# A routed block-sparse FFN on Trainium2: the last batch element routed one tile earlier, its scatters and the output gathers re-planned

## The chip, the cores and the metric

The kernel runs on one core of one Trainium2 chip. The metric is the time of the kernel on the device in microseconds (us). Three runs of the kernel before gave 1059.44, 1061.75 and 1058.58 us; the median is 1059.44. One further execution was recorded by the hardware profiler; all views below come from it.

## What is computed

The input x has 16 batch elements of 512 tokens with 512 features. Each element first goes through a conditional layer, then through a feed-forward network of which each token uses 4 of 16 blocks, and the result is added to x.

```python
# conditional layer; v = u = fside (rank 16), per batch element
z1 = einsum('bfi,bir->bfr', x, v[:, 0]) / inch
z  = einsum('bfr,bor->bfo', z1, u[:, 0]) / r
g  = gelu(x @ W.T + fc_bias + z + cond)          # exact gelu
# routed feed-forward network: 16 blocks of 128 hidden units
prob = softmax(g @ w_router + b_router)
mask = (one for each of the 4 largest of prob, else zero)   # 16 wide
h = relu(einsum('nd,ebd->neb', g, w1b) + b1b)
y = einsum('neb,ebd,ne->nd', h, w2b, mask) + b2
out = x + y
```

All of it is float32. A kernel need not compute the 12 blocks that a token doesn't use.

## The kernel before

**Two stages and two lists in HBM.** Stage 1 computes g for one batch element after the other, decides which four blocks each token takes, and writes each token's row of g (2 KB) four times into `g_d`, once into the list of each block that it takes. A place in a list is called a slot. Stage 2 walks over the lists in tiles of 128 slots (`T`): it fetches a tile of `g_d`, multiplies it with the weights of its one block, and writes 128 rows of results to `y_d` at the same slots. For each chunk of 128 tokens, it then gathers the four result rows of each token from `y_d`, adds them, b2 and x, and stores the output. There are 271 tiles (`NT` = 16 per element and 15 for lists that don't end on a tile's edge) and 64 chunks (four per element).

**Stage 1** is `window(b)` (line 578), one call per element b, in eight half steps h. In each, `cond_half` issues two of the element's 16 large products; between them stand the next element's preparation and the routing of the element before, a = b - 1: `logits_in`, `logits`, `route_in` (softmax's exponential), `route_a` to `route_c` (the four largest, their mask), `turn_g` (the four transposes of g that give token rows, into buffers `gr`), `rank` and `place` (the slot numbers). Larger table work is put in as chores (line 601). The scatters of element b - 2, 16 indirect DMAs from POOL's queue (GpSimd), are issued two per half step by `put` (line 445). Each waits for the product issued last before it (`after`, line 453), so that they are spread over the products.

**Stage 2** is the loop of line 782, one step i per tile. Its body issues `fetch(i + 4)`, `turn(i + 1)` (transposes the tile on TensorE), `first(i)` (product with w1, relu on ScalarE), `second(i - 1)` (product with w2, copy on ScalarE, store to `y_d`) and `pick(i + 2)` (VectorE copies the tile's weights out of `wall`), and then what a hand-made plan, the dictionary `work`, holds for step i. `plan(step, ...)` fills it (line 726). `mark[0]` is always the last product that `first` issued (line 656). The order of PE, VectorE and ScalarE is the order of the code; the queue of SP carries fetches, stores of y and stores of the output, ScalarE's queue the x loads, POOL's queue all scatters and gathers.

What the plan holds:

- The last element z = 15 has no later window, so its routing is planned over steps -1 to 5 (line 744). When all slots are known, `count` and `ends` work out the lists' lengths, two last table parts and `table` (steps 8 to 10) give the rows and blocks of tiles 22 and up.
- The scatters of elements 14 and 15 (line 751): 14's at steps 0 to 7, 15's at steps 8 to 15, two per step. Then five `put_zero` DMAs at steps 16 and 17 clear the ends of the lists.
- Tiles 0 to 21 (`AHEAD` = 22) are full tiles of the first four elements; their fetches don't wait for scatters of later elements (line 633). The fetch of tile 22, issued in step 18, waits for all scatters and zero writes.
- Output chunk n (1 to 64; `b`, `c` in the code) may be gathered when the tiles below `begun` = max(38, 4n + 15) are stored (line 677). Its first step `at` is at least `begun + 3` and at least 4 (`TOP_K`) after the chunk before (line 731): 4n + 37. At `at + j` stands `get_y` (line 691), gather j of four, into buffers `yg`; there are six, of two gathers each. From `at + 3` on follow `sum_b`, the sums `sum_y` and `sum_x` on VectorE at `at + 4` to `at + 7`, and the output store at `at + 7`. The x rows are loaded (`load_x`, line 682) at the step max(at - 24, soon), into 11 buffers `xa` and `xb`; a buffer is free when the output store of the chunk 11 earlier has landed. The last two elements' x stays in SBUF and is not loaded again.

A gather waits for its buffer and for the stores of y that its chunk needs (lines 700 to 703), and for nothing else.

Of the kernel before, what the change touches and what calls it, by code (L numbers as in the profile page):

```python
# [19 lines left out]
TOP_K = 4  # L20
# [5 lines left out]
def adaln_ffn_kernel(  # L26
# [31 lines left out]
    B, S, D = x.shape  # L58
# [8 lines left out]
    Q = 4  # L67
# [5 lines left out]
    NTC = -(-(NT - AHEAD) // P)  # L73
# [16 lines left out]
    SYNC = mybir.DependencyInfo(mybir.DependencyClass.Sync, mybir.DependencyReason.DATA)  # L90

    def alone(ins):

        tc.declare_no_dep(ins.ins, group="put_g", reason="disjoint rows of the lists")
        tc.declare_no_dep(ins.ins, group="get_g", reason="the tiles that run ahead are full")
        tc.add_to_no_dep_group("put_g", ins.ins)
# [158 lines left out]
    def cond_half(b, h):  # L255

        o = h // 2
        if h % 2 == 0:
            pms[o] = ps_m.tile([P, S], F32, tag="m", name=f"pc_{b}_{o}")
        for k in range(h % 2 * ND // 2, (h % 2 + 1) * ND // 2):  # L260
            ins = nc.tensor.matmul(  # L261
                pms[o], lhsT=wes[b][:, k, o * P : (o + 1) * P], rhs=xTs[b, k], start=(k == 0), stop=(k == ND - 1)
            )
        if h % 2:
            gelu(b, o, pms[o])
        return ins
# [178 lines left out]
    def put(b, c, j, after):  # L445

        ins = nc.gpsimd.indirect_dma_start(  # L447
            out=g_d[:, :],
            out_offset=bass.IndirectOffsetOnAxis(ap=slot[:, b, c, j : j + 1], axis=0),
            in_=grs[b, c].bitcast(I32),  # L450
            in_offset=None,
        )
        tc.add_manual_dep(ins.ins, after.ins.name, SYNC, reason="spread over the products")
        alone(ins)
        if b < Q:
            early.append(ins.ins)
# [42 lines left out]
    def put_zero(i, after):  # L499
        ins = nc.gpsimd.indirect_dma_start(  # L500
            out=g_blocks if i else g_d[:, :],
            out_offset=bass.IndirectOffsetOnAxis(ap=zero_i[:, i : i + 1], axis=0),
            in_=(zero if i else zero[:, 0:D]).bitcast(I32),
            in_offset=None,
            bounds_check=NSLOT // ZB - 1 if i else NSLOT - 1,
            oob_is_err=False,
        )
        tc.add_manual_dep(ins.ins, after.ins.name, SYNC, reason="spread over the products")
        alone(ins)
# [60 lines left out]
    chores = {Q + 1: [(fill,), (count, 0, True)], Q + 2: [(take,), (table_ahead,)]}  # L570
    for q in range(B // Q - 1):
        chores.setdefault(Q * q + Q + (3 if q == 0 else 1), []).append((count, q))
    parts_of = [(table_part, 1, i, h, B // Q) for h in range(B // Q) for i in range(NTC)]
    known = NTC * (B // Q - 1)
    for k in range(known):
        chores.setdefault(B - 2 + k // 3, []).append(parts_of[k])

    def window(b):
        a = b - 1
        do = [[] for _ in range(2 * ND)]  # L580
        if b + 1 < B:
            do[0] += [(weights, b + 1)]
            do[2] += [(turn_x, b + 1, 0), (turn_x, b + 1, 1)]
            do[4] += [(turn_x, b + 1, 2), (turn_x, b + 1, 3)]
            if b > 0:
                do[1] += [(logits_in, a)]
                do[3] += [(logits, a), (route_in, a)]
                do[4] += [(route, a)]
                do[5] += [(turn_g, a, 0), (turn_g, a, 1)]
                do[6] += [(turn_g, a, 2), (turn_g, a, 3)]  # L590
                do[7] += [(rank, a), (place, a)]
            if b + 2 < B:
                do[2] += [(spread_v, b + 2)]
                do[5] += [(turn_v, b + 2), (turn_v_out, b + 2)]
        else:
            do[0] += [(logits_in, a)]
            do[1] += [(logits, a), (route_in, a)]
            do[2] += [(turn_g, a, 0), (turn_g, a, 1), (route, a)]
            do[3] += [(turn_g, a, 2), (turn_g, a, 3)]
            do[5] += [(rank, a), (place, a)]  # L600
        for h, what in zip((1, 3, 6), chores.get(b, ())):
            do[h] += [what]
        for h in range(2 * ND):
            ins = cond_half(b, h)
            for what, *args in do[h]:
                what(*args)
            if b > 1:
                for j in (0, 1):
                    put(b - 2, h // 2, h % 2 * 2 + j, ins)
            if later:  # L610
                what, *args = later.pop(0)
                what(*args)
# [4 lines left out]
    rows, gts, wcs, gss, hTs, mark, stores = {}, {}, {}, {}, {}, {}, []  # L617
# [59 lines left out]
    def begun(b, c):  # L677

        n = b * NC + c + 1
        return max(AHEAD + E, n * PB // NC + E - 1)  # L680
# [10 lines left out]
    def get_y(b, c, j):  # L691
        if j % 2 == 0:
            ygs[b, c, j // 2] = ygp.tile([P, 2, D], F32, tag="yg", name=f"yg_{b}_{c}_{j}")
        ins = nc.gpsimd.indirect_dma_start(  # L694
            out=ygs[b, c, j // 2][:, j % 2, :].bitcast(I32),
            out_offset=None,
            in_=y_d[:, :],
            in_offset=bass.IndirectOffsetOnAxis(ap=slot[:, b, c, j : j + 1], axis=0),
        )
        new = stores[begun(b, c - 1) if b + c > 0 else 0 : begun(b, c)]  # L700
        tc.declare_no_dep(ins.ins, group="put_y", keep=new, reason="later tiles have no slot of this chunk")
        for p in new:
            tc.add_manual_dep(ins.ins, p.name, SYNC, reason="its rows")
        tc.keep_in_program_order(ins)
        tc.add_to_no_dep_group("get_y", ins.ins)

# [14 lines left out]
    GAP = 3  # L721
# [4 lines left out]
    def plan(step, *what):  # L726
        work.setdefault(step, []).append(what)

    for b in range(B):
        for c in range(NC):  # L730
            at = max(begun(b, c) + GAP, at + TOP_K if b + c else 0)
            k = b * NC + c
            soon = FREE - 2 * XA + 2 * k if k < XA else FREE + 4 + k - XA
            plan(soon if k < XA + XB else max(at - 24, soon), load_x, b, c)
            for j in range(TOP_K):
                plan(at + j, get_y, b, c, j)
            plan(at + LAND, sum_b, b, c)
            for h in range(2):
                plan(at + LAND + 1 + 2 * h, sum_y, b, c, h)
                plan(at + LAND + 2 + 2 * h, sum_x, b, c, h)  # L740
            plan(at + LAND + 4, store, b, c)


    z = B - 1
    for step, *what in (
        (-1, logits_in, z), (0, logits, z), (0, route_in, z), (1, turn_g, z, 0), (1, turn_g, z, 1), (1, route_a, z),
        (2, route_b, z), (2, turn_g, z, 2), (3, route_c, z), (3, turn_g, z, 3), (4, rank, z), (5, place, z),
        (6, count, B // Q - 1), (7, ends), *((8 + k, *w) for k, w in enumerate(parts_of[known:])), (8 + NTC, table, 1),
    ):
        plan(step, *what)  # L750
    for i in range(NC * TOP_K):
        for k, b in enumerate((z - 1, z)):
            plan(8 * k + i // 2, lambda b, c, j: put(b, c, j, mark[0]), b, i // TOP_K, i % TOP_K)
    for i in range(1 + NZ):
        plan(16 + i // 3, lambda i: put_zero(i, mark[0]), i)

    ENG = mybir.EngineType
    with tc.manual_schedule(engines={ENG.PE, ENG.DVE, ENG.Activation}):
# [10 lines left out]
        for b in range(B):  # L769
            if 2 <= b + 2 < B:  # L770
                load(b + 2)
            window(b)
# [76 lines left out]
```

## Time and profile before

| what | value |
|---|---|
| three runs, median | 1059.44 us (1058.58 to 1061.75) |
| profiled execution | 1086.83 us, its span 1085.1 us |
| granted clock of TensorE, mean | 0.967 |
| busy share of the span: PE, PEld, DVE, ACT, POOL | 89%, 59%, 60%, 48%, 51% |
| DMA | 342.43 MB, 316 GB/s over the span |
| HBM read, written | 179.91 MB, 163.32 MB |
| first product of tile 0, of tile 22, of tile 270 | 392.01, 469.33, 1046.91 us |
| first gather of results, last one issued | 512.34, 1074.77 us |

PE is TensorE's products, PEld its weight loads, DVE is VectorE, ACT ScalarE, POOL GpSimd, SP the engine that only issues DMAs. PE's busy share overstates its work, since products are pipelined and their ends modelled. In a stage's row the DMA share is the mean busy share of the 16 DMA engines; it can come out a little above 1. "Idle before, releaser" behind a group of instructions tells how long its engine stood still just before them and what ended most of that. The chain is followed back from the last instruction, at each step to what released it; its lines give the start, the length and the instruction.

The three queues of DMAs in the page: SP's queue (fetches, y stores, output stores) took 48.1% of the engines' time over the span, POOL's (scatters, gathers) 33.6%, ACT's (x loads) 4.1%.

### The profile page before, as it was taken

How to read it: one execution, taken by the hardware profiler on the slowest of the kernel's cores; microseconds unless marked ns; L12 is line 12 of the kernel's file. 1: busy time of each engine (PE TensorE's matmuls, PEld its weight loads, DVE VectorE, ACT ScalarE, POOL GpSimd, SP SyncE). 2: the span in 40 equal slices, each digit the busy share in tenths (PEclk: the TensorE clock that was granted, in tenths of full speed). 3: DMA queues.
4: the chain of work that ended last, by engine and by line, in shares of the span. 5: the costliest groups of instructions: out<-in, count | busy, mean ns of one | idle time of the engine just before them, and what ended most of it. 6: DMA issues, size and time to landing. Idle time of an engine off the chain costs nothing.

```text
span 1085.1 us, 19007 instructions
## 1 busy us (share of the span) xinstructions
PE 970.9 (89%) x5320; PEld 639.3 (59%) x5320; DVE 648.0 (60%) x1450; ACT 518.8 (48%) x1006; POOL 550.3 (51%) x538
## 2 busy tenths in 40 slices
PE   5998988988999888789799999999999999999960
PEld 3544444544444455567577677677767777777740
DVE  4365667566556767323366666566666666666675
ACT  2333332342333434456466666566656566666640
POOL 2046666666666667500454445455444454444555
PEclk9999999999999988989899999999999999999985
DMA  9966667566654469988799999999999999999996
GB/s 301 332 230 216 224 215 261 208 225 242 226 223 179 170 224 318 358 265 272 259 382 405 394 388 403 391 394 395 395 397 401 395 396 398 380 405 398 392 354 211
DMA packets 161480, 342.43 MB, mean 316 GB/s; under 512 B 28723, under 2 KB 36951, under 8 KB 159046
## 3 DMA queue, kind: packets, MB, share of 16 engines
q1 hardware_dynamic: 110928, 188.53, 48.1%
q0 software_dynamic: 41856, 136.96, 33.6%
q10 hardware_dynamic: 8592, 15.73, 4.1%
q8 instruction: 44, 0.72, 0.3%
q14 instruction: 60, 0.49, 0.1%
HBM read 179.91 MB, written 163.32 MB: 316 GB/s over the span
## 4 chain that ended last, share of the span: by engine, by line
PE 58%; DMA 19%; DVE 8%; issue 5%; ACT 3%; POOL 2%; SPq 2%; another core or an unknown queue 2%; ACTq 1%; DVEq 0%; POOLq 0%
PE pc L261 17%; DMA gt<-g_d 14%; PE ph L656 14%; PE py L666 13%; PE pts L649 6%; PE ptx L248 2%; PE ptg L357 2%; PE pw L241 2%; PE pa L285 1%; ACT gs L650 1%; PE pl L294 1%; DVE xT L250 1%; DMA yg<-y_d,slot 1%; POOL g_d L447 1%
## 5 line engine op out<-in xcount | busy, mean ns | idle before, releaser
L694 POOL DMA_INDIRECT yg<-y_d,slot x256 | 283.1, 1106 | 338.0 <-DVE xr L715 163.8
L643 DVE COPY wcur<-wall 128x1028 f32 x271 | 193.0, 713 | 271.1 <-PE py L666 164.0
L447 POOL DMA_INDIRECT g_d<-gr,slot x256 | 254.3, 993 | 185.2 <-issue 65.8
L656 PE MATMUL ph<-gs,wcur 128*128 128x128 f32 x2168 | 293.7, 279 | 17.7 <-ACT gs L650 9.8
L666 PE MATMUL py<-wcur,h 128*128 128x512 f32 x542 | 281.2, 601 | 5.5 <-ACT h L660 4.8
L656 PEld LDWEIGHTS ph<-gs,wcur 128*128 128x128 f32 x2168 | 266.8, 194 | 26.6 <-ACT gs L650 17.4
L261 PE MATMUL pc<-xT,we 128*128 128x512 f32 x512 | 246.3, 608 | 0.0
L649 PEld LDWEIGHTS pts<-ident,gt 128*128 128x128 f32 x1084 | 134.9, 143 | 165.2 <-issue 108.8
L667 ACT COPY y<-py 128x512 f32<-128x512 f32 x271 | 159.2, 587 | 94.0 <-PE py L666 69.5
L650 ACT COPY gs<-pts 128x512 f32<-128x512 f32 x271 | 160.0, 590 | 85.0 <-DMA gt<-g_d 39.6
L649 PE MATMUL pts<-ident,gt 128*128 128x128 f32 x1084 | 165.6, 276 | 16.4 <-DMA gt<-g_d 14.3
L660 ACT ACTIVATE h<-ph,wcur 128x128 f32<-128x128 f32 x271 | 100.0, 369 | 89.6 <-PE ph L656 43.0
L261 PEld LDWEIGHTS pc<-xT,we 128*128 128x128 f32 x512 | 88.4, 192 | 88.7 <-issue 88.7
L270 ACT ACTIVATE gT<-pc,biasT 128x512 f32<-128x512 f32 x64 | 44.0, 688 | 158.0 <-PE pc L261 101.8
L712 DVE TENSOR_TENSOR yg<-yg 128x512 f32<-128x512 f32 x128 | 87.3, 682 | 8.2 <-DMA yg<-y_d,slot 6.8
L666 PEld LDWEIGHTS py<-wcur,h 128*128 128x128 f32 x542 | 83.2, 194 | 6.8 <-ACT h L660 5.1
L250 DVE COPY xT<-ptx 128x512 f32<-128x512 f32 x64 | 42.0, 686 | 60.4 <-PE ptx L248 27.8
L715 DVE TENSOR_TENSOR xr<-xr,yg 128x512 f32<-128x512 f32 x112 | 76.6, 684 | 0.0
L357 PE MATMUL ptg<-ident,gT 128*128 128x128 f32 x256 | 37.8, 281 | 27.1 <-issue 9.8
L357 PEld LDWEIGHTS ptg<-ident,gT 128*128 128x128 f32 x256 | 30.0, 143 | 50.5 <-issue 24.9
L243 DVE TENSOR_TENSOR we<-pw,wc 128x512 f32<-128x512 f32 x64 | 40.1, 683 | 23.9 <-PE pw L241 16.2
L248 PEld LDWEIGHTS ptx<-ident,x 128*128 128x128 f32 x256 | 31.3, 146 | 18.3 <-issue 14.9
(159 smaller groups left out, 511.2 us busy)
## 6 DMA issues: line engine op xcount, KB each, us to landing
gt<-g_d SPq DMA_DIRECT2D x271, 256.0 KB
y_d<-y SPq DMA_DIRECT2D x271, 256.0 KB
x<-in_x_dram SPq DMA_DIRECT2D x16, 1024.0 KB
xr<-in_x_dram ACTq DMA_DIRECT2D x56, 256.0 KB
out_dram<-xr SPq DMA_DIRECT2D x56, 256.0 KB
wall<-in_w1T_dram SPq DMA_DIRECT2D x16, 256.0 KB
wall<-in_w2T_dram SPq DMA_DIRECT2D x16, 256.0 KB
g_d<-gr,slot POOLq DMA_INDIRECT x256
```

The costliest lines, as they stand in the source:

```text
L261: ins = nc.tensor.matmul(pms[o], lhsT=wes[b][:, k, o * P : (o + 1) * P], rhs=xTs[b, k], start=(k == 0), stop=(k == ND - 1))
L357: nc.tensor.transpose(pt[:, k, :], gTs[b, k][:, c * P : (c + 1) * P], ident)
L447: ins = nc.gpsimd.indirect_dma_start(out=g_d[:, :], out_offset=bass.IndirectOffsetOnAxis(ap=slot[:, b, c, j : j + 1], axis=0), in_=grs[b, ...
L643: nc.vector.tensor_copy(wcs[i], wall_f[:, bass.DynSlice(w, WW)])
L649: nc.tensor.transpose(pt[:, k, :], gts[i][:, k * P : (k + 1) * P], ident)
L650: nc.scalar.copy(gs.rearrange("p k t -> p (k t)"), pt.rearrange("p k t -> p (k t)"))
L656: mark[0] = nc.tensor.matmul(ph, lhsT=wcs[i][:, k * P : (k + 1) * P], rhs=gss[i][:, k, :], start=(k == 0), stop=(k == ND - 1))
L660: nc.scalar.activation(h, ph, AF.Relu, bias=wcs[i][:, ND * P : ND * P + 1])
L666: nc.tensor.matmul(py, lhsT=hTs[i], rhs=wcs[i][:, ND * P + 4 : WW], start=True, stop=True)
L667: nc.scalar.copy(y, py)
L694: ins = nc.gpsimd.indirect_dma_start(out=ygs[b, c, j // 2][:, j % 2, :].bitcast(I32), out_offset=None, in_=y_d[:, :], in_offset=bass.Indir ...
L712: nc.vector.tensor_tensor(yg[:, 0, :], yg[:, 0, :], yg[:, 1, :], ALU.add)
```

## The change

- The routing of element 15 begins earlier: both logit steps and the exponential in step -1, the rest in steps 0 to 3, so that `place` comes in step 3 instead of 5; `count`, `ends`, the table parts and the table come one step earlier.
- The four scatters of element 14's first chunk are issued in the last window, in its last two half steps. The other 12 stand at steps 0 to 3, three per step. Element 15's stand at steps 4 to 11, the zero writes at steps 12 and 13.
- Of the six table parts that are done in windows 14 and 15, window 14 takes four instead of three; the fourth stands in half step 7.
- Chunks are at least 3 steps apart instead of 4, so `at` becomes max(4n + 18, 3n + 38); the four gathers of a chunk stand at `at`, `at`, `at + 1`, `at + 2`.
- Each gather waits in addition for the last product of `first` in its step.

```diff
-        chores.setdefault(B - 2 + k // 3, []).append(parts_of[k])
+        chores.setdefault(B - 2 + k // 4, []).append(parts_of[k])
...
-        for h, what in zip((1, 3, 6), chores.get(b, ())):
+        for h, what in zip((1, 3, 6, 7), chores.get(b, ())):
...
             if b > 1:
                 for j in (0, 1):
                     put(b - 2, h // 2, h % 2 * 2 + j, ins)
+                if b == B - 1 and h >= 6:
+                    for j in (0, 1):
+                        put(a, 0, h % 2 * 2 + j, ins)
...
             tc.add_manual_dep(ins.ins, p.name, SYNC, reason="its rows")
+        tc.add_manual_dep(ins.ins, mark[0].ins.name, SYNC, reason="spread over the products")
         tc.keep_in_program_order(ins)
...
-            at = max(begun(b, c) + GAP, at + TOP_K if b + c else 0)
+            at = max(begun(b, c) + GAP, at + 3 if b + c else 0)
...
-                plan(at + j, get_y, b, c, j)
+                plan(at + 3 * j // TOP_K, get_y, b, c, j)
...
-        (-1, logits_in, z), (0, logits, z), (0, route_in, z), (1, turn_g, z, 0), (1, turn_g, z, 1), (1, route_a, z),
-        (2, route_b, z), (2, turn_g, z, 2), (3, route_c, z), (3, turn_g, z, 3), (4, rank, z), (5, place, z),
-        (6, count, B // Q - 1), (7, ends), *((8 + k, *w) for k, w in enumerate(parts_of[known:])), (8 + NTC, table, 1),
+        (-1, logits_in, z), (-1, logits, z), (-1, route_in, z), (0, route_a, z), (0, turn_g, z, 0),
+        (1, route_b, z), (1, turn_g, z, 1), (1, turn_g, z, 2), (2, route_c, z), (2, turn_g, z, 3),
+        (3, rank, z), (3, place, z), (5, count, B // Q - 1), (6, ends),
+        *((7 + k, *w) for k, w in enumerate(parts_of[known:])), (7 + NTC, table, 1),
...
-        for k, b in enumerate((z - 1, z)):
-            plan(8 * k + i // 2, lambda b, c, j: put(b, c, j, mark[0]), b, i // TOP_K, i % TOP_K)
+        if i >= TOP_K:
+            plan((i - TOP_K) // 3, lambda b, c, j: put(b, c, j, mark[0]), z - 1, i // TOP_K, i % TOP_K)
+        plan(4 + i // 2, lambda b, c, j: put(b, c, j, mark[0]), z, i // TOP_K, i % TOP_K)
...
-        plan(16 + i // 3, lambda i: put_zero(i, mark[0]), i)
+        plan(12 + i // 3, lambda i: put_zero(i, mark[0]), i)
```

## The prediction

> **What bounds the kernel now.** I read the page's 40 slices first, then the busy time by stage, cut where the slices change, then the chain that ended last around each hole, then the timelines of POOL, ACT and SP. The stages (core 0: us, busy time and instructions of PE, PEld, DVE, ACT, POOL, then granted clock, DMA share, GB/s):
>
> ```profile
> 438.00:455.00 17.00, 16.89 (x106) 12.38 (x104) 5.10 (x7) 10.09 (x21) 12.26 (x12) 1.00 1.01 374
> 455.00:466.00 11.00, 0.85 (x4) 0.69 (x4) 0.70 (x1) 0.84 (x2) 0.01 (x1) 0.63 0.65 227
> 466.00:511.00 45.00, 45.00 (x284) 34.45 (x283) 13.52 (x20) 28.91 (x60) 0.00 (x0) 0.98 0.86 283
> 511.00:532.00 21.00, 13.06 (x68) 9.12 (x67) 4.06 (x6) 6.83 (x15) 11.79 (x12) 0.78 0.80 279
> ...
> 568.00:980.00 412.00, 400.58 (x2490) 294.70 (x2489) 258.91 (x400) 252.61 (x534) 199.55 (x179) 1.00 1.04 396
> 980.00:1047.00 67.00, 66.52 (x423) 49.92 (x422) 44.69 (x69) 43.65 (x91) 33.11 (x31) 1.00 1.04 389
> 1047.00:1086.00 39.00, 2.69 (x13) 1.38 (x11) 25.65 (x39) 2.13 (x4) 22.69 (x22) 0.56 0.74 237
> ```
>
> A tile is 14 matmuls. From 466 to 511 PE is full: a tile takes 2.19 us (first products of tiles 22 and 41 start at 469.33 and 510.96). From 568 to 980 it is 2490/14 = 178 tiles in 412 us, 2.32 each, and the DMA share is 1.04: the DMA engines set the pace there, at 396 GB/s, which is 0.917 MB per tile (fetch 256 KB, store 256, gather 256, a quarter of 256 each for output and x). Three holes remain. Two are in the chain (start, us, what):
>
> ```profile
> 452.70 0.96 POOL g_d L500
> 453.96 8.52 DMA g_d<-zero,zero_i
> 462.61 2.60 DMA gt<-g_d
> 465.34 1.09 PE pts L649 x4
> ...
> 519.69 0.57 ACT y L667
> 520.26 2.29 another core or an unknown queue
> 522.63 0.59 ACT gs L650
> 523.22 6.50 another core or an unknown queue x2
> 530.16 2.07 PE py L666 x2
> ```
>
> Hole 1: tile 22 may be fetched only when the last scatter and the five zero writes have landed; PE stands 10.1 us. Hole 2: when POOL may gather at last (512.34) it issues 12 gathers back to back, until its six buffers are full, and from the start of tile 44 to that of tile 46 it takes 15.4 us instead of 4.4: 11 us lost. Hole 3 is the tail, 38.2 us from the last tile's first product (1046.91) to the end: POOL still has 21 gathers, 1.34 us apart (1047.95 to 1074.77), and DVE sums behind them.
>
> ```profile
> L694 POOL DMA_INDIRECT yg<-y_d,slot x256 | 283.1, 1106 | 338.0 <-DVE xr L715 163.8
> ```
>
> So POOL's gathers wait mostly for free buffers, that is, for the written plan's sums at one chunk in four steps.
>
> **The change, part by part** (steps are tiles; T(i) is the start of tile i's first product).
>
> **Hole 1.** POOL must issue, after the last scatter of element 13 (395.05 us), the same 37 instructions as before: 4 + 12 of element 14, 16 of element 15, 5 zeros. Before they wait for planned tiles and end with an issue at 453.96, 59 us later. After, four come in window 15, twelve are allowed at three per tile, and element 15's start at tile 4 (its place() comes at step 3). The holds end at tile 11 (430.9) and tile 13 (437.5), ahead of POOL, so POOL's own pace decides: 1.27 us at its freest (386 to 398 us), 1.41 in the eight unwaited scatters from 416.07 to 427.4, beside DVE. That is 47 to 52 us, so 442 to 447. I take 1.41, because 33 of these (8.7 MB) and some 18 tiles' transfers (9.4 MB) in 46 us are 393 GB/s, the full DMA rate. Landing 8.52 and fetch 2.60 as shown: tile 22 at 458.3 instead of 465.3, **-7 us**. Ends: -10 (1.27; PE itself gets there at 455.2) and -3 (1.5).
>
> What else moves there costs nothing that I can see: the routing of element 15 is the same DVE and ACT work a step earlier (the 1.28 us table load of the exponential and the 0.59 us copy of the logits included; no SP transfer moves). PE has no product between the two logit steps now, which exposes about 1 us, but PE waited 2.23 us for DVE's first weight copies at 389.8 anyway, and one table part of 2.4 us leaves DVE just there for window 14, where DVE is busy 38.6 of 60 us (300 to 360). Counts, ends and table keep PE waiting some 9 us at tiles 8 to 13 and do so still. Bounds -3 to +3, taken 0.
>
> **Hole 2 and the dense stretch.** Gathers are now held to tiles, four in three steps, so the burst of 12 cannot form. But chunk n's gathers go to step max(4n+18, 3n+38): until chunk 20, step 98, the stage carries a chunk each three tiles. Per tile that is 512 KB + (1024 + 256 + 256)/3 = 1.049 MB, at 396 GB/s 2.64 us. Steps 41 to 50, before x loads resume, I take at 2.25: 20 us; 48 more make 127; together 147. Before, T(41) to T(98) was 139.8 with the stall in it. **+7 us**: the burst's 11 are won, and 18 are paid for bytes brought forward.
>
> Here a rule speaks against the change. The Trainium skill ("DMA: Bandwidth & Descriptors", "Where 436 GB/s comes from") says that between HBM and SBUF the HBM side binds, at about 358 GB/s per core. By it the dense stretch would take 2.93 us a tile, 14 us more, and nearly all the gain would be gone. The row shows 396 GB/s over 412 us, so I take the row. The same page ("Issuing engines are not separate DMA queues") says that transfers from every engine share the 16 DMA engines: that I keep, as gathers put beside the tiles are paid for in full here.
>
> **From step 98 on** the spacing is four steps as before: T(98) to T(222) took 288.7 us and stays. x loads end at step 222 instead of 238 (the last at 977.2), so 16 tiles run at the 2.20 of tiles 238 to 270 instead of 2.30: **-2 us**.
>
> **The tail.** Chunk 64's gathers stand at step 274 instead of 293. After the last tile only chunks 63 and 64 are left. The last y store goes out 4 us after T(270) (1050.8), lands in about 4 (3.97 in the chain at 515.72), four gathers put the last issue at +12, it lands in 4.2 to 5.1 (the chain's last two), two sums 1.4, and from the last output's issue to the end is 3.7 (1081.4 to 1085.1): 21.7 instead of 38.2, **-16.5 us**.
>
> **New waits.** (a) The hold on POOL: behind a held gather stand only later gathers; the sums on DVE wait for those, and behind the sums stand the weight copies that PE needs. From chunk 20 the plan leaves seven tiles from the last needed tile to its sum. That tile's store is issued 3.4 us after the next tile starts (850.85, 854.21), the second gather 1.3 behind the landing, and the sum's place on DVE is 2.6 into step +7: 18.8 us, so 14.1 for the two landings without any wait, about 16.5 before DVE's own slack is used up. From the trace's records of issue and completion, 540 to 980 us: store 6.5, gather 6.5 in the middle, 7.7 and 7.2 at the ninth tenth. Sum 13.0, bad cases 14.9. Taken +1.5, ends 0 and +12. (b) In the dense stretch an x load on ACT needs the buffer of the chunk 11 earlier, whose output store is planned only two steps before (13 before the change). Such stores land in about 7 us; two steps are 5.3. ACT's next copies for PE stand behind the load. ACT already waits 0.7 to 2 us at such loads (866.41, 875.66 in the chain). Ten chunks, about 2 us late at PE's end, of which 1.4 is the DMA pace already counted: taken +2, ends 0 and +10.
>
> **Sum**: -7 + 7 - 2 - 16.5 + 1.5 + 2 = -15 us, on the profiled execution's 1086.83 us (its span 1085.1 and 1.7 around it), 1.38%. The median of the runs, 1059.44, is 2.5% shorter than that execution; the same share gives -14.6: **1045 us**.
>
> **Rivals.** **The gathers come late (slower).** One mechanism: store landing plus gather landing passes 16.5 us, as gathers now start with no lead while before they ran some seven steps ahead. Then every chunk from 20 to 64 makes DVE, and so PE, wait. Against it: 13.0 measured. For it: before, nobody depended on these times, and denser traffic may lengthen them. At 17.2, 0.7 us by 45 chunks is +31.5: about 1075. It ends the gain from some 0.35 us per chunk on.
> **The bytes only move (small gain).** The lost time at 511 to 532 comes back as contention in the dense stretch, +10: 1055. For it: the share of 1.04 there; against: no such hole from 568 to 980.
> **It doesn't do what it says.** The scatters are issued earlier but their landings, and so tile 22, stay: -8 instead of -15, 1052. For it, the DMA share of 1.01 just ahead of hole 1; against it, 65% in the hole itself.
> **All costs at their low ends**, hole 1 at -10 and the routing at -3: -24.5, so 1035.5.
>
> **How the numbers follow.** Forecast (1038 to 1050) 0.45; the two small gains (1050 to 1056) 0.20; better than 1038 0.10; within 0.3% (3.2 us, about what a measurement of this kernel can tell from no change) 0.07; slower 0.18. Range 1034 to 1061. Faster 0.75, same 0.07, slower 0.18.
>
> **What would show it.** Right: the last zero write issued near 447 and PE's hole there at 3 us; no stall after the first gather; 2.6 us per tile and about 396 GB/s for some 48 tiles, then 2.32; some 22 us from the last tile to the end. Wrong: DVE rows of L712 waiting for yg in mid stage with PE behind them; ACT waiting long at L689 near tiles 50 to 80; a dense stretch well above 2.7 us a tile.

## The result, and the profile after

The changed kernel takes **1073.44 us** (median of six runs, 1067.87 to 1075.44), the kernel before 1060.45 us in the six runs beside it. The ratio is 1.0121, with a 95% interval of 1.0092 to 1.0150: 13 us slower, where 15 us faster was forecast. The profiled execution of the changed kernel took 1073.55 us, its span 1071.8.

One thing must be known before two profiles are compared. The profile of before that the prediction read took 1086.83 us, 27 us more than that kernel's median. The unchanged kernel, run and profiled again, took 1061.14 us (span 1059.4; `b_again` below). Over all runs the chips fall into two groups. On some the kernel before takes 1060 to 1062 us and tile 0 starts at about 375 us; on the others it takes 1089 to 1093 us and tile 0 starts at 395 us or later. I call them group 1 and group 2. The profile the prediction read looks like group 2 (1086.83 us, tile 0 at 392.0; its chip is not on record), the times it was scaled to look like group 1. So each stage is compared within a group. In us, from first products of tiles, one execution each, differences taken before rounding:

| stage | predicted | group 1: b_again, after | difference | group 2: the first profile, after_same_chip | difference |
|---|---|---|---|---|---|
| start to tile 0 | 0 | 374.7, 375.0 | +0.3 | 392.0, 396.3 | +4.3 |
| tile 0 to 22 | -7 | 74.6, 71.4 | -3.2 | 77.3, 74.9 | -2.4 |
| 22 to 41 | 0 | 41.6, 41.9 | +0.2 | 41.6, 41.6 | 0 |
| 41 to 98 | +7, and +2 for x loads | 131.3, 155.9 | **+24.6** | 139.8, 151.8 | +12.0 |
| 98 to 222 and 222 to 270 | -2, and +1.5 for late gathers | 398.0, 401.3 | +3.3 | 396.1, 403.6 | +7.5 |
| tile 270 to the end | -16.5 | 39.2, 26.3 | -12.8 | 38.1, 26.2 | -11.9 |
| sum | -15 | span 1059.4, 1071.8 | +12.4 | span 1085.1, 1094.4 | +9.4 |

The stages of b_again, in the columns of the prediction's first view (stretch, us, busy time and instructions of PE, PEld, DVE, ACT, POOL, granted clock, DMA share, GB/s):

```profile
419.00:433.00 14.00, 14.00 (x95) 10.84 (x93) 4.97 (x7) 9.53 (x20) 10.95 (x11) 1.00 1.03 386
433.00:446.00 13.00, 2.04 (x10) 1.24 (x9) 0.70 (x1) 1.11 (x3) 0.62 (x1) 0.69 0.61 225
491.00:511.00 20.00, 20.00 (x131) 15.26 (x130) 10.20 (x16) 13.30 (x29) 14.92 (x14) 1.00 0.94 342
511.00:622.00 111.00, 107.31 (x669) 78.84 (x668) 69.58 (x108) 68.02 (x144) 55.37 (x50) 1.00 1.04 397
...
1020.00:1033.00 13.00, 2.99 (x13) 1.46 (x11) 11.57 (x19) 2.12 (x4) 10.25 (x10) 0.70 0.98 336
1033.00:1046.00 13.00, 0.00 (x0) 0.00 (x0) 8.76 (x14) 0.00 (x0) 10.26 (x9) 0.50 0.83 235
```

The same stages of the changed kernel:

```profile
417.00:430.00 13.00, 13.00 (x86) 9.84 (x85) 4.18 (x6) 8.67 (x18) 10.26 (x10) 1.00 1.03 383
430.00:443.00 13.00, 2.72 (x12) 1.92 (x11) 0.70 (x1) 1.47 (x3) 0.95 (x1) 0.63 0.66 232
489.00:509.00 20.00, 20.00 (x131) 15.26 (x130) 11.10 (x17) 13.18 (x28) 13.80 (x12) 1.00 0.95 336
509.00:645.00 136.00, 116.27 (x672) 86.16 (x672) 83.66 (x129) 68.85 (x144) 67.67 (x63) 0.92 1.00 362
645.00:940.00 295.00, 280.56 (x1738) 205.97 (x1737) 182.85 (x282) 178.37 (x373) 133.29 (x125) 0.99 1.04 390
...
1045.00:1058.00 13.00, 3.25 (x14) 1.65 (x12) 8.45 (x13) 2.36 (x5) 4.68 (x6) 0.73 0.80 278
```

Three things are to be seen. The hole ahead of tile 22 (second row of each) is there in both. In b_again the first gathers (third row) leave PE full: the 11 us stall that the prediction called hole 2 is not there to be won. And the dense stretch of the changed kernel (509 to 645) moves less per second than the same tiles before, 362 against 397 GB/s, with PE's clock at 0.92: something stands still there, and PE with it (116.27 us busy of 136, against 107.31 of 111). The chain of waits of the changed kernel shows what (start, length, what; ACTq is ScalarE's sequencer):

```profile
526.53 0.66 DVE yg L716
527.19 7.36 DMA out_dram<-xr
534.55 0.03 ACTq L692
...
534.62 0.33 ACTq L692
...
535.05 0.59 ACT gs L653
...
535.69 2.08 PE ph L659 x8
...
545.10 7.91 DMA out_dram<-xr
553.01 0.03 ACTq L692
```

L692 is `load_x`. ScalarE issues the x load of chunk 14 when the output store of chunk 3, whose buffer it takes, has landed; its copy `gs` for the next tile stands behind the load, and PE behind that. ScalarE's waits between 489 and 645 us (waiting engine and line, releaser: us in all, times, longest):

```profile
ACT gs L653 <- DMA out_dram<-xr: 22.3, 5, 4.8
```

In b_again no wait of ScalarE for an output store is among the groups of that stretch.

### The profile page after: what moved, and what is told of

It reads as the page before. It is cut to its first block, busy times and chain, and to the rows that moved or that the text cites. A ratio compares the mean times of both kernels' runs of the same rounds, so it can differ in the third digit from the quotient of the medians.

```text
span 1071.8 us, 19107 instructions
## 1 busy us (share of the span) xinstructions
PE 968.5 (90%) x5320; PEld 640.9 (60%) x5320; DVE 648.2 (60%) x1450; ACT 521.0 (49%) x1006; POOL 542.8 (51%) x538
## 4 chain that ended last, share of the span: by engine, by line
PE 62%; DMA 21%; DVE 10%; issue 2%; POOL 1%; ACT 1%; SPq 1%; ACTq 1%; DVEq 0%; POOLq 0%
PE pc L261 17%; PE ph L659 16%; PE py L669 14%; DMA gt<-g_d 12%; PE pts L652 7%; DMA out_dram<-xr 3%; PE ptx L248 2%; DMA y_d<-y 2%; PE pw L241 2%; DVE xT L250 2%; PE pa L285 2%; DMA yg<-y_d,slot 1%; PE ptg L357 1%; PE pl L294 1%; DVE ti L326 1%
## 5 line engine op out<-in xcount | busy, mean ns | idle before, releaser
L697 POOL DMA_INDIRECT yg<-y_d,slot x256 | 275.4, 1076 | 356.5 <-DMA y_d<-y 130.5
L659 PE MATMUL ph<-gs,wcur 128*128 128x128 f32 x2168 | 295.6, 280 | 31.1 <-ACT gs L653 20.3
L659 PEld LDWEIGHTS ph<-gs,wcur 128*128 128x128 f32 x2168 | 269.7, 196 | 38.3 <-ACT gs L653 31.9
L653 ACT COPY gs<-pts 128x512 f32<-128x512 f32 x271 | 159.4, 588 | 81.8 <-DMA out_dram<-xr 22.3
L652 PE MATMUL pts<-ident,gt 128*128 128x128 f32 x1084 | 165.9, 276 | 21.6 <-DMA gt<-g_d 20.3
L716 DVE TENSOR_TENSOR yg<-yg 128x512 f32<-128x512 f32 x128 | 87.9, 686 | 71.7 <-DMA yg<-y_d,slot 71.5
L357 PE MATMUL ptg<-ident,gT 128*128 128x128 f32 x256 | 36.8, 277 | 15.6 <-DVE gr L359 12.8
```

Source lines behind the costliest of these rows:

```text
L357: nc.tensor.transpose(pt[:, k, :], gTs[b, k][:, c * P : (c + 1) * P], ident)
L652: nc.tensor.transpose(pt[:, k, :], gts[i][:, k * P : (k + 1) * P], ident)
L653: nc.scalar.copy(gs.rearrange("p k t -> p (k t)"), pt.rearrange("p k t -> p (k t)"))
L659: mark[0] = nc.tensor.matmul(ph, lhsT=wcs[i][:, k * P : (k + 1) * P], rhs=gss[i][:, k, :], start=(k == 0), stop=(k == ND - 1))
L697: ins = nc.gpsimd.indirect_dma_start(out=ygs[b, c, j // 2][:, j % 2, :].bitcast(I32), out_offset=None, in_=y_d[:, :], in_offset=bass.Indir ...
L716: nc.vector.tensor_tensor(yg[:, 0, :], yg[:, 0, :], yg[:, 1, :], ALU.add)
```

## The experiments

The reading after the first comparison: the start and the tail gave something, the stretch 41 to 98 took more than both. Four causes were weighed for that loss: ScalarE waiting at x loads; the hold that ties gathers to tiles, so that results come late (the prediction's main rival); bytes brought forward into a stretch that the DMA engines pace, paid for in full (theory C in the expectations); and the place of an x load within a chunk's steps (theory D). A ratio is to the kernel before on the same chip. A number on a single stage comes from one profiled execution, and a cut in a piece of code is marked by dots.

### The same kernel again: b_again

No edit. 

> The kernel before, unchanged, for a second profiled execution. Theory A (the first profiled execution of it, 26 us over the median, had 17 us of its own in stage 1 and 11 at the first gathers, which ordinary executions don't have): the new profile spans 1056 to 1062 us, tile 0 starts at 375 to 377 us instead of 392, no stall of 11 us follows the first gathers, and tile 270 starts near 1020. Theory B (the stall at the first gathers belongs to the kernel, profiling only stretches it): a stall of 8 us or more again within tiles 42 to 47. Time against the kernel before: 1.000.

Measured 1060.98 us, ratio 1.0006 [0.9992, 1.0020], span 1059.4. From tile 41 to 50 a tile takes 2.19 us while 12 gathers are issued back to back (492.12 to 507.87). The stall after the first gathers is not a constant part of this kernel.

### The earlier start alone: start_only

The change without its hold and without its new spacing of gathers:

```diff
-        tc.add_manual_dep(ins.ins, mark[0].ins.name, SYNC, reason="spread over the products")
...
-            at = max(begun(b, c) + GAP, at + 3 if b + c else 0)
+            at = max(begun(b, c) + GAP, at + TOP_K if b + c else 0)
...
-                plan(at + 3 * j // TOP_K, get_y, b, c, j)
+                plan(at + j, get_y, b, c, j)
```

> The kernel before with only the earlier routing and scatters; gathers 4 steps apart and without the hold, as before. Theory A (the start gains what was forecast, the loss lies wholly with the gathers): -6 to -8 us, ratio 0.993 to 0.9945. Rival (the earlier scatters only collide with the tiles, so the start gains nothing in ordinary runs): ratio 0.999 to 1.003.

Measured 1057.52 us, ratio 0.9960 [0.9948, 0.9972]: 3 to 4 us won, where 6 to 8 were expected. Stretch 41 to 98 takes 130.6 us and the tail 38.4, as before. So the loss is wholly in what was left out here.

### The x loads later: loads_later, loads20, loads22

The change with x loads planned later; its own step is at - 24. loads_later: `max(at - 18, soon + 6)`; loads20: `max(at - 20, soon)`; loads22: `max(at - 22, soon)`.

> The changed kernel with the x loads from the 12th chunk on six steps later (at - 18 instead of at - 24), so that the output store whose buffer they take was planned 8 steps before and not 2. Theory A (ACT standing some 4 us at each such load costs the dense stretch 9 to 10 us beyond its bytes): no ACT stalls of 4 us at tiles 50 to 80, tiles 41 to 98 in 147 us instead of 156, and 8 to 10 us faster than the changed kernel, ratio to the kernel before about 1.004. Rival (the stretch is bound by the gathers' hold or by the DMA rate anyway): within 3 us of the changed kernel, ratio 1.010 to 1.014.

> The changed kernel with the x loads four steps later (at - 20), which keeps their place in the chunk's cycle of four steps; the output store whose buffer they take is then planned 6 steps before. Theory C (moved bytes: five chunks' gathers and stores and four x loads brought ahead of tile 222 cost their 7.6 MB at 396 GB/s, 19 us, whatever ACT waits for; waits are on top, some 10 us): tiles 41 to 222 in 444 to 448 us instead of 451, time 3 to 6 us under the changed kernel. Theory A (ACT's waits are the larger part): tiles 41 to 222 in 436 to 440 us, 11 to 14 us under the changed kernel.

> The changed kernel with x loads at step at - 22 instead of at - 24, as loads20 has them at at - 20 and loads_later at at - 18. If ScalarE's waits at the x loads are what the change loses in its dense stretch, and each step of delay takes some 2.6 us off each of five waits of about 4 us, two steps take nearly all: some 1062 to 1066 us, ratio 1.000 to 1.006, as loads20. If the place of a load within the four steps of a chunk decides (at - 22 and at - 18 stand at the same place, at - 24 and at - 20 at the other), it stays slow as loads_later did: 1071 to 1076, ratio 1.010 to 1.015, with tiles 98 to 222 taking over 300 us.

| | ratio | 41 to 98 | 98 to 222 |
|---|---|---|---|
| after (at - 24) | 1.0121 [1.0092, 1.0150] | 155.9 | 295.0 |
| after_same_chip (at - 24), group 2 | 1.0106 [1.0067, 1.0145] | 151.8 | 295.3 |
| loads22, group 2 | 1.0138 [1.0109, 1.0166] | 144.2 | 308.1 |
| loads20 | 1.0017 [0.9998, 1.0036] | 143.3 | 291.9 |
| loads_later (at - 18) | 1.0113 [1.0080, 1.0146] | 142.9 | 306.5 |

All three take 8 to 13 us out of the dense stretch, each compared within its group. ScalarE's waits for output stores, 22.3 us in the changed kernel, are all but gone in loads20 (489 to 633 us):

```profile
ACT gs L653 <- DMA out_dram<-xr: 0.2, 1, 0.2
```

The trace of loads20 has chunk 14's load 1.74 us behind the landing of its buffer's output store (533.35, 535.09); in the changed kernel it is 0.07 (534.55, 534.62). Two of them lose it again later, between tiles 98 and 222: those with loads at - 18 and at - 22, so their times hardly fall. loads20 takes 435.2 us from tile 41 to 222, just under the 436 to 440 expected if ScalarE's waits are the larger part of the loss.

### The same on one chip: after_same_chip, loads20_same_chip

after and loads20 had run on different chips.

> The changed kernel itself, on the same chip as loads20_same_chip, because the two were so far timed on different chips. Its place in tiles 41 to 98: some 14 us more than the kernel before needs, or more. Ratio 1.009 to 1.016 if the loss doesn't depend on the chip.

> As loads20: x loads four steps later than in the change, and nothing else. If ScalarE standing at the loads for the output stores of eleven chunks earlier is worth 10 us or more of the change's loss, it is 8 to 14 us below after_same_chip, on whatever chip. If the first result came from the chip, it is within 4 us of it.

Group 2: 1103.57 us, ratio 1.0106 [1.0067, 1.0145], against 1095.84 us, 1.0040 [1.0019, 1.0062]. The later loads are worth 7.7 us there, just under what was expected; stretch 41 to 98 falls from 151.8 to 143.9. (The two profiled spans are both 1094.4; loads20's execution started tile 0 4.7 us later.)

### The place of the load alone: phase22

The kernel before with x loads at - 22. 

> The kernel before with the x loads two steps later (at - 22) and nothing else: their place in the chunk's cycle of four steps becomes that of the run with at - 18, which had no long ACT waits and yet gained nothing. Theory D (that place costs the four-step stretch its 12 to 15 us): tiles 98 to 222 in 300 to 306 us instead of 290, ratio 1.009 to 1.014. Rival (the place has no effect, the loss needs the changed gathers): ratio 0.999 to 1.002.

Ratio 1.0011 [0.9990, 1.0032]; 98 to 222 takes 291.4 us. By itself the place does nothing: theory D falls in that form. Together with the change's gathers it costs 12 to 15 us (308.1 against 296.0 in loads20_same_chip, 306.5 against 291.9 in loads20). In loads_later PE waited 13.5 us there for DVE's weight copies, ten times, and those stand behind sums that waited for gathers. Why two loads' places do this and three (at - 24, - 20, - 16) don't is open.

### The hold: no_hold, l20_free, slack

no_hold is the changed kernel without its new dependence in `get_y`, l20_free is loads20 without it. slack keeps it and moves all sums and stores three steps later (`LAND` from 3 to 6), x loads to at - 16.

> The changed kernel without the gathers' wait for the product of their tile; spacing 3 and the early start stay. Theory A (the hold makes gathers late, DVE waits 62 us in total for them, of which some 6 us reach PE; the dense bytes and ACT's waits stay): 3 to 8 us faster than the changed kernel, ratio about 1.005 to 1.009. Rival (the hold is the whole loss): ratio 0.985 to 0.995. Second rival (the hold does good, since it stops the burst): slower than the changed kernel, ratio 1.015 and up.

> The changed kernel with x loads at at - 20 and without the hold: early start and spacing 3 are left of the change. If the hold costs by itself (late gathers keep DVE, and so PE): 3 to 6 us under the run with at - 20 and the hold, ratio to the kernel before 0.996 to 0.999. If the hold is harmless: within 2 us of it, 1.000 to 1.003. If the hold helps: above 1.004.

> The changed kernel with x loads at at - 20 and without the hold of gathers to tiles, on another chip. If the hold is harmless, as the runs with more slack say, it is within 0.3% of loads20, ratio 0.999 to 1.005. If the hold is needed to keep gathers off the tiles, as its first try on the slower chip (1.015) would have it, ratio 1.010 to 1.020.

> The changed kernel with the sums three steps later (LAND 6 instead of 3) and the x loads at at - 16, so that neither DVE waits for gathers that are held to their tile nor ACT for output stores. Theory C (bytes): tiles 41 to 222 still take 438 to 443 us, some 19 over the 421 of the kernel before; with a tail that is some 5 us longer, the time is 3 to 8 us under the changed kernel. Theory A (waits): tiles 41 to 222 in 423 to 430 us, 15 us or more under the changed kernel.

no_hold: 1071.43 us in four runs, ratio 1.0120 [1.0072, 1.0167]. None of its three expectations came true, and in group 1 it can't be told from the changed kernel (1.0121). slack: 1062.03 us, 0.9999 [0.9983, 1.0016], as loads20. In the changed kernel DVE waits for gathers:

```profile
DVE yg L716 <- DMA yg<-y_d,slot: 71.5, 51, 4.8
```

In loads20 this group is 84.2 us, with slack 7.5, and the two take the same time. So in group 1 DVE's waits for gathers stay in its own slack. An effect of the hold on the time could not be told there; no_hold's interval leaves room for 5 us either way.

In group 2 it does something. l20_free took 1106.0 us, ratio 1.0149 [1.0081, 1.0218], and again 1103.32, 1.0106 [1.0073, 1.0140]; with the hold 1.0040. The stall at the first gathers is back. From tile 41 to 50, 19.7 us at full pace, all five group 2 executions without the hold and with the first gather in step 41 took 27.6 to 31.1 us, the three with it 19.7 to 20.2. The chain of a stall (dense_late_again) goes through ScalarE's waits and names no releaser:

```profile
526.69 0.59 ACT gs L653
527.27 3.00 another core or an unknown queue x2
...
530.57 0.58 ACT y L670
531.15 3.42 another core or an unknown queue
```

In the trace both waits end on the semaphore that TensorE's products raise, at 530.28 and 534.57 us, while the last products before them end, as modelled, at 528.49 and 532.29. So ScalarE waits for TensorE, which is about 2 us late each time; what holds TensorE is open.

So the prediction's hole 2 exists, and the hold closes it, but only in group 2, and the measured time is one of group 1.

### Fewer tiles dependent on the start: ahead28

start_only with `AHEAD = 28`: tile 28 is the first whose fetch waits for all scatters. 

> The early start alone with 28 instead of 22 tiles that may run before all scatters have landed. The hole of 10 us at tile 22 should be gone (28 tiles take PE past the last landing). Theory C (from the first gathers on DMA sets the pace, so the hole gives back only the bytes that move while it would stand): 3 to 7 us under the early start alone, ratio to the kernel before 0.989 to 0.993. Rival (all ten us come through): ratio 0.986 and below. Rival (the gathers start six steps later, and that eats it): 0.996 and up.

1058.49 us, ratio 0.9977 [0.9963, 0.9991]. Most of the hole is gone: tile 41 is reached 7.2 us sooner after tile 0 than in start_only, and some 6 us are still lost between tiles 22 and 28 (19.1 us instead of 13.4). The tail grows from 38.4 to 46.0, since the gathers now begin six tiles later, which was one of the two rivals. What the start gains, the end gives back.

### The dense stretch at the end: dense_late

start_only with three steps per chunk for the last 19 chunks only:

```diff
-            at = max(begun(b, c) + GAP, at + TOP_K if b + c else 0)
+            at = max(begun(b, c) + GAP, at + (TOP_K if b * NC + c < 45 else 3) if b + c else 0)
```

> The early start alone, and of the gathers only the spacing of 3 for chunks 46 to 64 (no hold): the last chunk ends at step 274 as in the changed kernel, but the five chunks are brought forward at the end of the list walk, far from the first x loads. Theory C (bytes are paid wherever they are put): tile 270 starts some 15 us later than with the early start alone (near 1033), the tail is 11 to 14 us shorter, time 0 to +4 us against the early start alone, ratio to the kernel before 0.996 to 1.000. Rival (only the place was wrong): tile 270 at 1018 to 1022 and a ratio of 0.984 to 0.988.

> The same kernel as dense_late, on another chip, beside best_again. If its gain is a matter of the plan, ratio 0.990 to 0.996; if it came from the one chip, 0.997 to 1.002.

Group 1: **1054.34 us, ratio 0.9928 [0.9909, 0.9947]**, the lowest ratio of all versions and between its two expectations. The tail is 25.0 us instead of 38.4 in start_only (another chip of group 1). The price, from tile 222 to 270, first start_only and then dense_late:

```profile
910.30:1017.88 107.58, 106.17 (x670) 79.30 (x669) 70.17 (x109) 68.81 (x144) 52.73 (x49) 1.00 1.04 394
```

```profile
913.15:1028.64 115.49, 108.17 (x668) 80.22 (x669) 80.26 (x126) 69.66 (x145) 67.53 (x61) 0.99 1.04 395
```

3.2 MB more at the same rate (115.49 us at 395 GB/s less 107.58 at 394) make some 8 us; 7.9 were measured, and 2.2 more between 98 and 222. In group 2 the gain shrinks to 0.9979 [0.9955, 1.0002], not told from none.

### All together: best

start_only with `AHEAD = 28`, three steps from chunk 40 on, x loads at - 20.

> The early start, 28 tiles that may run ahead, no hold, spacing 4 up to chunk 39 and 3 from chunk 40 on (last chunk at step 274), x loads at at - 20: what the runs before point to. Theory C (bytes brought forward cost least where the x loads have ended, and the time won at tile 22 is given back only in the tail, which this cuts): tile 41 at 107 us after tile 0, tiles 41 to 222 in 421 to 426, tail 24 to 27 us, 1046 to 1050 us, ratio 0.986 to 0.990. Rival (the tail's gain is paid in full by the bytes again): 1054 to 1057, ratio 0.994 to 0.997.

> The same kernel as best, on another chip: the earlier start alone, tile 22 replaced by tile 28 as the first tile whose fetch waits for all scatters, spacing of three steps only from chunk 40 on, x loads at step at - 20. Theory C (bytes brought forward into the stretch that the DMA engines pace are paid for in full; moved to the end, where x loads have stopped, they cost less than the tail gains): the gain at the start, 7 us at tile 41 beside the earlier start alone, and that of the late spacing, 3 us, add up: tile 0 near 375 us, no standing still of ScalarE at the first gathers, 1047 to 1053 us where the kernel before takes 1060, ratio 0.988 to 0.993. Rival (the chip of the first try was only slow, and the two parts don't add up): 1056 to 1060, ratio 0.997 to 1.0.

> As best: it gained nothing on two chips on which the kernel before takes 1089 to 1093 us. If this chip is again such a one: ratio 0.998 to 1.003. If it is one on which the kernel before takes 1060 us and the plan's gains add up: 0.985 to 0.993.

All three landed on group 2 chips: 0.9990 [0.9960, 1.0020], 1.0018 [0.9995, 1.0041], 1.0001 [0.9977, 1.0026]. There is no gain there, and the expected one did not come; against phase22, its stages show a stall of some 7 us at the first gathers in place of the one of 8, 12 to 19 us more from tile 160 to 270, and 11 to 14 us won in the tail. None of them ran on a chip of group 1, so whether the gains add up there is open.

## Why the prediction was wrong

Between the forecast of -15 and the measured +12.4 (spans, group 1) lie 27.4 us. Two terms of the sum make 21.6 of them.

**Hole 2, -11 inside the +7: the failing step in group 1.** The prediction took a stall of one profiled execution, 27 us longer than the median, for a part of the kernel, and scaled the sum to the median by its share. In group 1 the stall is 0 (b_again), and all of the 11 us was missing. A check was at hand: 1086.83 against three runs within 3 us of 1059.44 said that this execution held some 27 us which the others did not. In group 2 this step holds: tiles 41 to 50 take 19.7 us instead of 30.7. The change loses there all the same, by the terms that follow; its +12.0 from tile 41 to 98 is -11.0 for the stall, +7.9 for the x loads and +15.1 for the rest.

**(b) x loads, +2: measured 12.6 (155.9 less 143.3) in group 1, 7.9 in group 2. This is the second failing step, and nearly as large: the mechanism was right, its size was not.** The place was named too, tiles 50 to 80, but the price was taken near the low end of 0 to 10. By the prediction's own figures, ten chunks at 2 us less 1.4, it would have been 6. An output store lands in 7 to 8 us there and two steps take 5.5; ScalarE stood 22.3 us for such landings, in five waits of up to 4.8, and 12.6 us came through to PE, since the copies behind each load feed PE's next tile.

**Bytes, +18: measured +12.0, with the wrong judgement of what they buy.** loads20 shows the bytes without ScalarE's waits. Tiles 41 to 98 in b_again, then in loads20:

```profile
490.94:622.27 131.33, 127.64 (x801) 94.43 (x800) 80.08 (x124) 81.63 (x172) 70.56 (x63) 1.00 1.02 388
```

```profile
489.32:632.64 143.32, 128.71 (x801) 93.64 (x799) 95.42 (x145) 83.22 (x172) 81.25 (x75) 1.00 1.03 389
```

That is 51.0 and 55.7 MB: 12 gathers, 3 output stores and 4 x loads more. 4.7 MB at 389 GB/s are 12.2 us; 12.0 were measured. Of the 6 us that the forecast had too much, 3.7 are the stretch itself (147 against 143.3), and 2.5 the kernel before, which takes 131.3 us without the stall and not 128.8. The row against the 358 GB/s of the Trainium skill ("DMA: Bandwidth & Descriptors", "Where 436 GB/s comes from") was the right one to take. But b_again's rows 1020 to 1046 show what those bytes did before: 336 GB/s at a share of 0.98, then 235 at 0.83. The tail's first 26 us were not idle, they moved these bytes. So -12.8 in the tail is bought for +12.0. Theory C carries this part.

**The tail, -16.5: measured -12.8 and -11.9.** Its length was to be 21.7 and is 26.3. The last store of y goes out at 1052.69, 7.2 us after tile 270's first product instead of 4: it stands on SP behind an output store that waits for DVE's sums. SP's timeline in the changed kernel:

```profile
1047.49 1.89 SPq L671 DMA_DIRECT2D y_d<-y  x2
1052.12 0.34 SPq L722 DMA_DIRECT2D out_dram<-x  x1
1052.69 0.33 SPq L671 DMA_DIRECT2D y_d<-y  x1
```

That is 3.2 of the 4.6 us; the prediction did not follow SP's queue there.

**Hole 1, -7: measured -3.2 and -2.4.** The changed side was right in group 1: the last zero write goes out 55.0 us after tile 0, in the predicted window (50 to 55). What was off is the other side: in b_again it goes out after 57.6 us, not after 62.0 as in the first profile. Both kernels run into the hole with the DMA engines full (386 and 383 GB/s), which would leave little to win; no run here tests that. The chain at the hole, b_again and then the changed kernel:

```profile
432.29 10.13 DMA g_d<-zero,zero_i
...
442.54 2.52 DMA gt<-g_d
```

```profile
429.99 8.35 DMA g_d<-zero,zero_i
...
438.47 2.70 DMA gt<-g_d
```

**Late gathers, +1.5.** As a rival this fell: DVE's waits are there (71.5 us), but slack takes them away without a gain. It is not quite nothing: with loads at - 18, PE comes to stand behind DVE (13.5 us). From tile 98 to 270 the changed kernel takes 3 to 7 us more than the kernel before, where -0.5 was predicted; loads20 takes 397.6 and slack 402.3, so this is near what single executions differ by, and not settled. (Inside the -2, the x loads end with tile 219 and not 222, which leaves the term as it is.)

**The rivals.** The slower one, gathers that come late, named about 1075 us, and 1073 were measured: that is luck, since its mechanism is not what the time went to. "The bytes only move" was nearest in effect, since it took 10 of hole 2's 11 us away, but in group 1 there was no stall whose time could come back. In group 1 the change is then -2.6 up to tile 41, +12.0 for bytes, +12.6 for x loads, +3.3 from tile 98 to 270 and -12.8 in the tail: 12.5 by these rounded terms, 12.4 measured.

## What to carry to other kernels

Before a stall of a single profiled execution is put into a sum, compare that execution's time with the runs: a surplus over them may sit in just that stall, and ordinary runs then don't have it to win. A tail of transfers was worth little more here than what its DMA share left idle; its bytes, moved into a stretch that the DMA engines already pace, were paid for at that pace. When a plan packs stores and the loads that reuse their buffers closer together, count the steps between them against the landing time, and look at what else stands behind the waiting load on its engine.

## What the runs showed of the hardware

- Chips differ by 30 us for one and the same kernel: medians of before were 1060.67 and 1061.55 us on two of them, 1089.64 on a third, 1093.02 and 1092.55 in two series on a fourth. The difference is 17 us or more ahead of tile 0 and 8 to 11 at the first gathers; from tile 98 to 222 they agree (289.9 us in b_again, 288.7 in the first profile, 291.4 in phase22). The cause was not found.
- An x load is also held by the DMAs ahead of it. In the trace, this program's SP and ScalarE DMAs take turns on eight semaphores. Between tiles 98 and 222 of b_again all 31 x loads were issued just after the landing of the DMA before them on their semaphore, each time a fetch (0.02 us after it in the median, 0.10 at most); ScalarE stood 35.7 us at them in all. So with transfers of about 7 us a queue that looks free made the engine that issues a load wait, for a transfer that the load doesn't need.
